# Mixing and layer 1 of a graph network: score products in halves of the array, W1 centred, shared places, fewer products behind each hyperedge block

## Chip, cores and metric

The kernel runs on one core of one Trainium2 chip. The metric is the device time of one execution in microseconds. Fast executions of the same kernel mostly agree within about 0.3%, so a difference of a few microseconds needs several rounds of both kernels on the same chip. For engines I use the names of the profile: PE (TensorE), DVE (VectorE), ACT (ScalarE), POOL (GpSimd), SP (the engine that issues most loads and stores here).

## The reference, cut to what matters

Eight batches of 2048 nodes with 64 features pass through four residual layers, each followed by a layernorm. The change touches the end of layer 0 and layer 1:

```python
# layer 0, hypergraph attention: industry = (adj / deg) @ (x @ W_ind); g = a mix over hyperedges
def attn_scores(f):
    return jnp.tanh(f @ fcW + fcb) @ av
pair = jnp.stack([industry, g], axis=2)
coefs2 = jax.nn.softmax(attn_scores(pair), axis=-1)
out = jnp.einsum('bnk,bnkf->bnf', coefs2, pair)
x = _layernorm(x + out)
# layer 1
A_td = A + jnp.eye(n); dinv = jax.lax.rsqrt(jnp.sum(A_td, axis=1))
H = jnp.einsum('bmd,nm->bnd', X, dinv[:, None] * A_td * dinv[None, :])
x = _layernorm(x + jnp.einsum('bnd,kd->bnk', H, W))
```

I call the choice between `industry` and `g` **mixing**. A softmax over two entries needs only the difference of the two scores.

## The kernel before

Batches lie in pairs: 128 partitions hold two batches of 64 features, so there are NP = 4 pairs, and 2048 nodes make NCH = 4 column groups of 512. Mixing therefore has 16 steps. PE's instructions are kept in program order. A generator, `filler`, gives the big adjacency products one by one, and `fill(n)` places n of them between the small products of a latency-bound stage: first behind the hyperedge blocks, then in mixing. It yields 576 products for layer 0 and then 640 for layer 1.

```python
# hyperedge stage: 57 blocks (t, s), three products each, seven fillers behind each
pz = pps.tile([P, C], F32, tag="mm", name="pz", bufs=3)
for i, (l, r) in enumerate(((ident_r, both[0]), (ident_r, both[1]), (ohs[s], tab2))):
    mm(pz, lhsT=l, rhs=r, start=i == 0, stop=i == 2)
if s == 0 and t + 1 < NT:
    fill(3)
    now = begin(t + 1)
fill(7)
...
def mix_parts(i):
    ...
    mm(pi, lhsT=bd_ind, rhs=ut, start=True, stop=True)           # 128 x 512, float32
    nc.vector.tensor_tensor(inds[i], pi, inv_row[:, cols(c)], ALU.mult)
    ...                                                          # pg: four transposes of g
    nc.scalar.activation(gts[i], pg, AF.Identity, bias=-1.0)

def mix_scores(i):
    for b in range(2):
        t1 = []
        for src in (inds[i], gts[i]):
            mm(pf, lhsT=fcz[:, b, :], rhs=src, start=True, stop=True)  # half of fcz's rows are zero
            nc.scalar.activation(t1[-1], pf, AF.Tanh, bias=fcb_col)
        nc.gpsimd.tensor_tensor(t1[0], t1[0], t1[1], ALU.subtract)
        tts[i].append(t1[0])

def mix_weigh(i):
    for b in range(2):
        mm(pd, lhsT=avz[:, b, :], rhs=tts[i][b], start=b == 0, stop=b == 1)  # half of avz's columns are zero
    nc.scalar.activation(th, pd, AF.Tanh, scale=0.5)
    nc.vector.tensor_tensor(ind, ind, gt, ALU.subtract)
    nc.vector.scalar_tensor_tensor(ind, th, 1.0, ind, op0=ALU.add, op1=ALU.mult)
    nc.vector.scalar_tensor_tensor(ind, ind, 0.5, gt, op0=ALU.mult, op1=ALU.add)

def mix_end(i):
    ...                                # pt: four transposes, add x, layernorm, store x1
def l1_parts(p, c):                    # layer 1's input, scaled and split in two float32r parts
    nc.vector.tensor_tensor(y, y, dinv[:, wide(c), None].to_broadcast([P, JT, P]), ALU.mult)
    part[c] = split(lp, y, f"v{c}", 1, [P, JT, P])
...
for i in range(steps + 1):
    k = 10 if i > NCH else 8
    ...                                # parts(i), weigh(i-1), scores(i), end(i-1), fill(k) after each
    if i == NCH:                       # the rest of layer 0's products, then start layer 1
        for _ in filler:
            pass
        ...
```

## Time and profile before

| | before |
|---|---|
| median of three runs, us | 2214.5 |
| PE busy, share of the span | 89% |
| DVE / ACT / POOL busy | 50% / 18% / 21% |
| stretch that the change touches | about 88 to 655 us |

A share of busy time is an average over stages. The prediction below therefore reads the stages one by one; it explains the columns of its rows where they first appear.

### The profile page before, as it was taken

To read this page: it belongs to the slowest core of one execution; us is meant where nothing else is said; L and a number is where in the kernel's file an instruction comes from. 1 tells how busy PE (TensorE), PEld (TensorE's weight loads), DVE (VectorE), ACT (ScalarE), POOL (GpSimd) and SP (SyncE) were. 2 spreads that over 40 slices of the span, in tenths; PEclk is the share of its full clock that TensorE was granted. 3 is DMA by queue.
4 is the path that set the end of the run, shared out by engine and by line. 5 is a ranking of instruction groups with operands and counts; after the bars stand their busy time and mean duration, and the time that the engine had idled before them with its cause. 6 is when DMAs were issued, how large, how long until landed. Compare 5 with 4: busy or idle time off the path is not lost. (4 is left out here: it accounts for less than half of the span.)

```text
span 2213.6 us, 19723 instructions
## 1 busy us (share of the span) xinstructions
PE 1972.6 (89%) x7292; PEld 1277.5 (58%) x7292; DVE 1112.3 (50%) x1825; ACT 405.9 (18%) x794; POOL 474.8 (21%) x420
## 2 busy tenths in 40 slices
PE   5799889898849999799999999999896999989994
PEld 3577656565634444474465456456445786877773
DVE  5579746666432232218846864772783233332322
ACT  1355433323111111010010010001001112212110
POOL 2368623434223333100100110110110010110102
PEclk8799989999869999999999999999998999999997
DMA  7823333231300000100000000000001112121110
GB/s 261 278 78 100 114 108 109 93 99 63 114 12 0 19 19 19 43 1 8 8 5 5 10 5 3 8 10 0 10 5 42 39 26 56 39 52 39 47 30 21
DMA packets 73241, 110.59 MB, mean 50 GB/s; under 512 B 26784, under 2 KB 35008, under 8 KB 70512
## 3 DMA queue, kind: packets, MB, share of 16 engines
q1 hardware_dynamic: 62304, 73.66, 11.3%
q0 software_dynamic: 5088, 25.89, 3.4%
q10 hardware_dynamic: 5744, 9.70, 1.2%
q8 instruction: 59, 0.97, 0.2%
q14 instruction: 46, 0.38, 0.1%
HBM read 79.27 MB, written 29.95 MB: 49 GB/s over the span
## 5 line engine op out<-in xcount | busy, mean ns | idle before, releaser
L1048 PE MATMUL py<-wp,xg 128*128 128x512 f32 x1024 | 448.4, 597 | 8.5 <-DVE fcav L1053 5.8
L1048 PEld LDWEIGHTS py<-wp,xg 128*128 128x128 f32 x1024 | 193.6, 191 | 254.4 <-issue 215.9
L173 PE MATMUL u<-adj,hi 128*128 128x512 f32 x768 | 256.7, 416 | 0.0
L173 PE MATMUL u<-adj,lo 128*128 128x512 f32 x768 | 247.5, 402 | 0.0
L995 PE MATMUL u<-pt,xn 128*128 128x512 f32 x512 | 227.9, 603 | 9.0 <-DVE u L1004 7.8
L1053 DVE TENSOR_TENSOR fcav<-py,emb_n 128x512 f32<-128x512 f32 x256 | 177.1, 692 | 51.9 <-PE py L1048 37.0
L1054 DVE TENSOR_REDUCE r<-fcav 128x32 f32<-128x512 f32 x256 | 175.4, 685 | 8.1
L995 PEld LDWEIGHTS u<-pt,xn 128*128 128x128 f32 x512 | 97.2, 193 | 131.4 <-issue 114.7
L678 PE MATMUL u<-adj,vh 128*128 128x512 f32 x512 | 158.2, 408 | 14.6 <-ACT vh L168 10.8
L173 PEld LDWEIGHTS u<-adj,hi 128*128 128x128 f32 x768 | 143.4, 190 | 40.9 <-issue 11.2
L173 PEld LDWEIGHTS u<-adj,lo 128*128 128x128 f32 x768 | 145.1, 191 | 34.0
L1056 POOL TENSOR_TENSOR r<-r,bias 128x256 f32<-128x256 f32 x32 | 23.4, 730 | 634.9 <-DVE r L1054 634.9
L156 POOL TENSOR_TENSOR ln_r<-ln_e,neg_half 128x8 f32<-128x8 f32 x64 | 106.9, 1670 | 223.4 <-DVE ln_e L154 219.5
L678 PE MATMUL u<-adj,vl 128*128 128x512 f32 x512 | 152.1, 398 | 0.0
L989 DVE TENSOR_SCALAR pt<-pt 128x512 f32<-128x512 f32 x64 | 48.8, 780 | 173.2 <-ACT pt L988 171.7
L1144 DVE SCALAR_TENSOR_TENSOR fcav<-fcav,ar 128x512 f32<-128x512 f32 x64 | 44.3, 692 | 177.4 <-ACT ar L1143 177.2
L678 PEld LDWEIGHTS u<-adj,vh 128*128 128x128 f32 x512 | 96.1, 189 | 45.0 <-ACT vh L168 12.3
L993 POOL TENSOR_TENSOR acc<-acc,pt 128x512 f32<-128x512 f32 x60 | 79.6, 1327 | 163.8 <-DVE pt L989 161.0
L1126 POOL TENSOR_TENSOR r<-r,xn 128x512 f32<-128x512 f32 x16 | 20.5, 1280 | 433.8 <-DVE r L1125 433.8
L678 PEld LDWEIGHTS u<-adj,vl 128*128 128x128 f32 x512 | 96.4, 189 | 22.1 <-issue 0.7
L150 ACT ACTIVATE r<-ln_c 128x512 f32<-128x512 f32 x64 | 40.3, 630 | 264.5 <-DVE ln_c L146 249.6
L1143 ACT CAST ar<-fcav 128x512 fp32r<-128x512 f32 x64 | 39.7, 621 | 213.8 <-DMA fcav<-in_adj_t 144.8
(342 smaller groups left out, 2736.6 us busy)
## 6 DMA issues: line engine op xcount, KB each, us to landing
adj<-in_adj_t POOLq DMA_DIRECT2D x16, 1024.0 KB, 8.2
fcav<-in_adj_t SPq DMA_DIRECT2D x64, 256.0 KB, 2.9
x_hbm<-r SPq DMA_DIRECT2D x28, 256.0 KB, 2.1
hs_hbm<-st ACTq DMA_DIRECT2D x16, 292.0 KB, 5.6
xt<-in_x_t SPq DMA_DIRECT2D x16, 256.0 KB, 4.6
xc<-in_x_n SPq DMA_DIRECT2D x16, 256.0 KB, 2.9
u_hbm<-ut SPq DMA_DIRECT2D x16, 256.0 KB, 2.5
gn<-gs_hbm SPq DMA_DIRECT2D x16, 256.0 KB, 3.7
```

Of the source, the lines that this page charges most:

```text
L150: nc.scalar.activation(r, xc, AF.Square)
L156: nc.gpsimd.tensor_tensor(rstd, vare, neg_half[:, :groups], ALU.pow)
L173: tc.keep_in_program_order(nc.tensor.matmul(*args, **kw))
L678: nc.tensor.matmul(u[c], lhsT=half[:, j, :], rhs=adj[t][:, cols(c)], start=t == 0 and i == 0, stop=ends and not own,)
L989: nc.vector.tensor_scalar(pt, pt, 1.0, None, op0=ALU.max)
L993: nc.gpsimd.tensor_tensor(acc, acc, pt, ALU.add)
L995: nc.tensor.matmul(u[p], lhsT=xn[p][:, t, :], rhs=pt, start=t == 0, stop=t == NT - 1)
L1048: nc.tensor.matmul(py.rearrange("p o d -> p (o d)"), lhsT=xg[b][:, q, cols(j, P)], rhs=wp[:, q, cols(k)], start=q == 0, stop=q == 1,)
L1053: nc.vector.tensor_tensor(pr, py, e_b, ALU.mult)
L1054: nc.vector.tensor_reduce(r[:, j, b, cols(k, OH)], pr, AX.X, ALU.add)
L1143: nc.scalar.copy(ar, a)
L1144: nc.vector.scalar_tensor_tensor(a, a, 1.0, ar.bitcast(F32), op0=ALU.mult, op1=ALU.not_equal, accum_out=left[:, t, k:k + 1],)
```

## The change

Its intent: less PE time for the scores, and fewer holes in mixing.

- `pf` uses 64 rows of the array for each batch of a pair, and `pd` 64 columns, so that the two batches' products can run side by side.
- Five instead of seven fillers stand behind each hyperedge block; the others remain for mixing. The last two tiles change places.
- The columns of W1 are centred, so that what layer 1 adds has mean zero, and its layernorm needs no mean.
- Three passes go from DVE to POOL: ind - gt, the addition of g (now to x and early, as x + g, called the residual below), the scaling of layer 1's input. The factor of one half goes into the DVE pass that adds the residual. The copies of `ut` that DVE made go to ACT.
- Loads of mixing get a pool of their own, opened before the hyperedge stage ends; layer 1 uses the places of layer 0's split parts and can start quarter by quarter.

```diff
@@ layernorm: with centred=True no mean, no subtraction
@@ hyperedge stage
-        for t in range(NT):
+        tiles = [*range(NT - 2), NT - 1, NT - 2]
+        for k, t in enumerate(tiles):
...
-                fill(7)
+                fill(5)
@@ mixing
-        ut = mp.tile([P, C], F32, tag="ut0", name="ut0", bufs=2)
+            uts[i] = mp0.tile([P, C], F32, tag="ut0", name="ut0", bufs=2)
...
+        nc.gpsimd.tensor_tensor(rs[i], rs[i], gn, ALU.add)
 
     def mix_scores(i):
-        for b in range(2):
-            t1 = []
-            for src in (inds[i], gts[i]):
+        t1 = []
+        for src in (inds[i], gts[i]):
+            for b in range(2):
+                s = slice(b * F, (b + 1) * F)
-                mm(pf, lhsT=fcz[:, b, :], rhs=src, start=True, stop=True)
+                mm(pf, lhsT=fc2[s, :], rhs=src[s, :], start=True, stop=True)
...
+        for b in range(2):
+            nc.gpsimd.tensor_tensor(t1[b], t1[b], t1[2 + b], ALU.subtract)
+        tts[i] = t1[0:2]
+        nc.gpsimd.tensor_tensor(inds[i], inds[i], gts[i], ALU.subtract)
 
     def mix_weigh(i):
-            mm(pd, lhsT=avz[:, b, :], rhs=tts[i][b], start=b == 0, stop=b == 1)
+            mm(pd[b * F:(b + 1) * F, :], lhsT=av2, rhs=tts[i][b], start=True, stop=True)
-        nc.vector.tensor_tensor(ind, ind, gt, ALU.subtract)
-        nc.vector.scalar_tensor_tensor(ind, th, 1.0, ind, op0=ALU.add, op1=ALU.mult)
-        nc.vector.scalar_tensor_tensor(ind, ind, 0.5, gt, op0=ALU.mult, op1=ALU.add)
+        nc.vector.scalar_tensor_tensor(inds[i], th, 1.0, inds[i], op0=ALU.add, op1=ALU.mult)
@@ layer 1: w1_m is the mean of each row of bd_w1's blocks
+        nc.vector.tensor_scalar(bd_w1[s, s], bd_w1[s, s], w1_m[s], None, op0=ALU.subtract)
-        nc.vector.tensor_tensor(y, y, dinv[:, wide(c), None].to_broadcast([P, JT, P]), ALU.mult)
-        part[c] = split(lp, y, f"v{c}", 1, [P, JT, P])
+        nc.gpsimd.tensor_tensor(y, y, dinv[:, wide(c), None].to_broadcast([P, JT, P]), ALU.mult)
+        part[p, c] = split(va, y, f"v{c}", 1, [P, JT, P])
@@ the order of a step: scores(i), end(i-1), load and ind and g of i+1, weigh(i), fill(k) after each
-        k = 10 if i > NCH else 8
+        k = 9 if i > NCH else 8
-        if i == NCH:
-            for _ in filler:
-                pass
```

More of the change, by code (lines that the diff above doesn't have):

```diff
@@ L139, in to_rows, with layernorm @@
         return t
-    def layernorm(pool, r, dst, groups=2 * JT):
-        mean = pool.tile([P, groups], F32, tag="ln_m", name="ln_m", bufs=2)
-        nc.vector.tensor_reduce(mean, r, AX.X, ALU.add)
+    def layernorm(pool, r, dst, groups=2 * JT, centred=False):
         xc = pool.tile([P, groups, F], F32, tag="ln_c", name="ln_c", bufs=1)
-        nc.vector.scalar_tensor_tensor(
-            xc, mean[:, :, None].to_broadcast([P, groups, F]), -1.0 / F, r,
-            op0=ALU.mult, op1=ALU.add,
-        )
-        nc.scalar.activation(r, xc, AF.Square)
+        if centred:
+            squares, xc = xc, r
+        else:
+            mean = pool.tile([P, groups], F32, tag="ln_m", name="ln_m", bufs=2)
+            nc.vector.tensor_reduce(mean, r, AX.X, ALU.add)
+            nc.vector.scalar_tensor_tensor(
+                xc, mean[:, :, None].to_broadcast([P, groups, F]), -1.0 / F, r,
+                op0=ALU.mult, op1=ALU.add,
+            )
+            squares = r
+        nc.scalar.activation(squares, xc, AF.Square)
         var = pool.tile([P, groups], F32, tag="ln_v", name="ln_v", bufs=2)
-        nc.vector.tensor_reduce(var, r, AX.X, ALU.add)
+        nc.vector.tensor_reduce(var, squares, AX.X, ALU.add)
         vare = pool.tile([P, groups], F32, tag="ln_e", name="ln_e", bufs=2)
@@ L190, in tile_gnn_fast @@
     fcav = const.tile([P, 2, 2, P], F32, name="fcav")
-    fcz, avz = fcav[:, 0], fcav[:, 1]
+    fc2, av2 = fcav[:, 0, 0], fcav[:, 0, 1, 0:F]
     bd_ind = const.tile([P, P], F32, name="bd_ind")
@@ L273, in tile_gnn_fast @@
     xc, part = {}, {}
+    mixed, free = set(), set()
     def fetch(p, c):
@@ L338, in products @@
                             yield
+                    if p == NP - 1 and g == 1 and t % JT == JT - 1:
+                        first_parts(t // JT, free)
                     if p + 1 < NP and t % JT == JT - 1:
@@ L354, in fill, with first_parts @@
         for _ in range(n):
-            next(filler, None)
+            if next(filler, None) == "wait":
+                break
+    def first_parts(c, where):
+        where.add(c)
+        if c in mixed and c in free:
+            l1_parts(0, c)
     ph_scope = ExitStack()
@@ L398, in tile_gnn_fast @@
             nc.gpsimd.dma_start(dst, v.rearrange("(n o) -> n o", o=1))
-        for t in (fcz, bd_ind):
-            nc.gpsimd.memset(t, 0.0)
+        nc.gpsimd.memset(bd_ind, 0.0)
         for b in range(2):
             s = slice(b * F, (b + 1) * F)
-            nc.gpsimd.dma_start(fcz[s, b, :], fc_w)
+            nc.gpsimd.dma_start(fc2[s, :], fc_w)
             nc.gpsimd.dma_start(bd_ind[s, s], w_ind)
-        nc.gpsimd.memset(avz, 0.0)
         age = hy.tile([P, F], F32, name="age")
@@ L519, in tile_gnn_fast @@
         nc.vector.scalar_tensor_tensor(order, po[:, 0, :], float(P), olo, op0=ALU.mult, op1=ALU.add)
-        for b in range(2):
-            s = slice(b * F, (b + 1) * F)
-            nc.vector.tensor_copy(avz[:, b, s], av_col.to_broadcast([P, F]))
+        nc.vector.tensor_copy(av2, av_col.to_broadcast([P, F]))
         so_scope.close()
@@ L622, in tile_gnn_fast @@
         for b in range(2):
+            s = slice(b * F, (b + 1) * F)
             pf = pps.tile([P, 2, P], F32, tag="sm", name="pf", bufs=2)
-            mm(pf, lhsT=fcz[:, b, :], rhs=het, start=True, stop=True)
+            mm(pf, lhsT=fc2[s, :], rhs=het[s], start=True, stop=True)
             nc.scalar.activation(tf[:, b], pf, AF.Tanh, bias=fcb_col)
@@ L665, in tile_gnn_fast @@
         ta_scope.close()
+    mix_scope = ExitStack()
+    mp0 = mix_scope.enter_context(tc.tile_pool(name="mix0", bufs=1, side="right"))
     def product(pool, psum, chunk, plus_identity=False):
@@ L696, in begin @@
         def begin(t):
-            fetch_rows(t + 2)
+            k = tiles.index(t)
+            for ahead in tiles[k + 2:k + 3]:
+                fetch_rows(ahead)
             hrow = hrows.pop(t)
@@ L717, in begin @@
             return S, both, ohs, R, co
+        tiles = [*range(NT - 2), NT - 1, NT - 2]
         now = begin(0)
-        slots(1, pps, "mm", 3)
-        for t in range(NT):
+        slots(tiles[1], pps, "mm", 3)
+        for k, t in enumerate(tiles):
             S, both, ohs, R, co = now
@@ L727, in tile_gnn_fast @@
                     mm(pz, lhsT=l, rhs=r, start=i == 0, stop=i == 2)
-                if s == 0 and t + 1 < NT:
+                if s == 0 and k + 1 < NT:
                     fill(3)
-                    now = begin(t + 1)
-                fill(7)
-                if s == max(0, S - 5) and t + 2 < NT:
-                    slots(t + 2, pps, "mm", 3)
+                    now = begin(tiles[k + 1])
+                fill(5)
+                if s == max(0, S - 5) and k + 2 < NT:
+                    slots(tiles[k + 2], pps, "mm", 3)
                 z = pz.rearrange("p (b f) -> p b f", f=F)
@@ L768, in tick, with mix_load, mix_ind, mix_g @@
             pending.pop(0)[1]()
-    mix_scope = ExitStack()
+    lp_scope = ExitStack()
+    lp = lp_scope.enter_context(tc.tile_pool(name="l1", bufs=1))
     mp = mix_scope.enter_context(tc.tile_pool(name="mix", bufs=1, side="right"))
-    inv_row = mp.tile([P, N], F32, name="inv_row")
-    nc.scalar.dma_start(inv_row, inv_hbm[:])
     lps_scope = ExitStack()
     lps = lps_scope.enter_context(tc.tile_pool(name="l1_ps", bufs=1, space=PSUM))
+    bd_w1 = on_diagonal(lp, w1_t, "bd_w1")
+    w1_m = lp.tile([P, 1], F32, name="w1_m")
+    nc.vector.tensor_reduce(w1_m, bd_w1, AX.X, ALU.add)
+    nc.vector.tensor_scalar(w1_m, w1_m, 1.0 / F, None, op0=ALU.mult)
+    for b in range(2):
+        s = slice(b * F, (b + 1) * F)
+        nc.vector.tensor_scalar(bd_w1[s, s], bd_w1[s, s], w1_m[s], None, op0=ALU.subtract)
     def wide(c):
         return slice(c * JT, (c + 1) * JT)
-    gts, inds, tts = {}, {}, {}
-    def mix_parts(i):
+    uts, invs, gts, inds, tts, rs = {}, {}, {}, {}, {}, {}
+    xn, done = [], [0] * NP
+    steps = NP * NCH
+    def mix_load(i):
+        if i < steps:
+            p, c = divmod(i, NCH)
+            uts[i] = mp0.tile([P, C], F32, tag="ut0", name="ut0", bufs=2)
+            nc.sync.dma_start(uts[i], u0_hbm[p][:, cols(c)])
+            invs[i] = mp0.tile([P, C], F32, tag="inv0", name="inv0", bufs=2)
+            nc.sync.dma_start(invs[i], inv_hbm[:, cols(c)])
+    def mix_ind(i):
+        pi = lps.tile([P, C], F32, tag="mm", name="pi", bufs=4)
+        mm(pi, lhsT=bd_ind, rhs=uts.pop(i), start=True, stop=True)
+        inds[i] = mp.tile([P, C], F32, tag="ind", name="ind", bufs=3)
+        nc.vector.tensor_tensor(inds[i], pi, invs.pop(i), ALU.mult)
+    def mix_g(i):
         p, c = divmod(i, NCH)
@@ L788, in mix_parts @@
         )
-        ut = mp.tile([P, C], F32, tag="ut0", name="ut0", bufs=2)
-        nc.sync.dma_start(ut, u0_hbm[p][:, cols(c)])
-        pi = lps.tile([P, C], F32, tag="mm", name="pi", bufs=4)
-        mm(pi, lhsT=bd_ind, rhs=ut, start=True, stop=True)
-        inds[i] = mp.tile([P, C], F32, tag="ind", name="ind", bufs=2)
-        nc.vector.tensor_tensor(inds[i], pi, inv_row[:, cols(c)], ALU.mult)
+        rs[i] = mp.tile([P, JT, P], F32, tag="r", name="r", bufs=2)
+        load_x(rs[i], p, c)
         pg = lps.tile([P, C], F32, tag="mm", name="pg", bufs=4)
@@ L799, in mix_parts @@
         nc.scalar.activation(gts[i], pg, AF.Identity, bias=-1.0)
+        nc.gpsimd.tensor_tensor(rs[i], rs[i], gn, ALU.add)
     def mix_scores(i):
-        tts[i] = []
-        for b in range(2):
-            t1 = []
-            for src in (inds[i], gts[i]):
+        t1 = []
+        for src in (inds[i], gts[i]):
+            for b in range(2):
+                s = slice(b * F, (b + 1) * F)
                 pf = lps.tile([P, C], F32, tag="mm", name="pf", bufs=4)
-                mm(pf, lhsT=fcz[:, b, :], rhs=src, start=True, stop=True)
+                mm(pf, lhsT=fc2[s, :], rhs=src[s, :], start=True, stop=True)
                 t1.append(mp.tile([P, C], F32, tag="t1", name="t1", bufs=4))
                 nc.scalar.activation(t1[-1], pf, AF.Tanh, bias=fcb_col)
-            nc.gpsimd.tensor_tensor(t1[0], t1[0], t1[1], ALU.subtract)
-            tts[i].append(t1[0])
+        for b in range(2):
+            nc.gpsimd.tensor_tensor(t1[b], t1[b], t1[2 + b], ALU.subtract)
+        tts[i] = t1[0:2]
+        nc.gpsimd.tensor_tensor(inds[i], inds[i], gts[i], ALU.subtract)
     def mix_weigh(i):
@@ L817, in mix_weigh @@
         for b in range(2):
-            mm(pd, lhsT=avz[:, b, :], rhs=tts[i][b], start=b == 0, stop=b == 1)
+            mm(pd[b * F:(b + 1) * F, :], lhsT=av2, rhs=tts[i][b], start=True, stop=True)
         th = mp.tile([P, C], F32, tag="th", name="th", bufs=1)
         nc.scalar.activation(th, pd, AF.Tanh, scale=0.5)
-        ind, gt = inds[i], gts[i]
-        nc.vector.tensor_tensor(ind, ind, gt, ALU.subtract)
-        nc.vector.scalar_tensor_tensor(ind, th, 1.0, ind, op0=ALU.add, op1=ALU.mult)
-        nc.vector.scalar_tensor_tensor(ind, ind, 0.5, gt, op0=ALU.mult, op1=ALU.add)
+        nc.vector.scalar_tensor_tensor(inds[i], th, 1.0, inds[i], op0=ALU.add, op1=ALU.mult)
     def mix_end(i):
         p, c = divmod(i, NCH)
-        r = mp.tile([P, JT, P], F32, tag="r", name="r", bufs=2)
-        load_x(r, p, c)
+        r = rs.pop(i)
         pt = lps.tile([P, C], F32, tag="mm", name="pt", bufs=4)
@@ L832, in mix_end @@
             transpose(pt[:, cols(j, P)], inds[i][:, cols(j, P)])
-        nc.vector.tensor_tensor(r, pt.rearrange("p (t f) -> p t f", f=P), r, ALU.add)
+        nc.vector.scalar_tensor_tensor(
+            r, pt.rearrange("p (t f) -> p t f", f=P), 0.5, r, op0=ALU.mult, op1=ALU.add
+        )
         layernorm(mp, grouped(r), grouped(r))
         nc.sync.dma_start(x1_hbm[p][:, wide(c), :], r)
+        if p == 0:
+            first_parts(c, mixed)
     def l1_parts(p, c):
-        y = lp.tile([P, JT, P], F32, tag="y", name="y", bufs=2)
+        y = staged("y")
         nc.sync.dma_start(y, x1_hbm[p][:, wide(c), :])
-        nc.vector.tensor_tensor(y, y, dinv[:, wide(c), None].to_broadcast([P, JT, P]), ALU.mult)
-        part[c] = split(lp, y, f"v{c}", 1, [P, JT, P])
+        nc.gpsimd.tensor_tensor(y, y, dinv[:, wide(c), None].to_broadcast([P, JT, P]), ALU.mult)
+        part[p, c] = split(va, y, f"v{c}", 1, [P, JT, P])
     def l1_end(p, c, ut):
@@ L846, in l1_end @@
             mm(po[:, j, :], lhsT=ut[:, cols(j, P)], rhs=bd_w1, start=True, stop=True)
-        x1 = lp.tile([P, JT, P], F32, tag="y", name="x1", bufs=2)
+        x1 = staged("x1")
         nc.sync.dma_start(x1, x1_hbm[p][:, wide(c), :])
@@ L852, in l1_end, with load_xn @@
         if p == NP - 1:
-            layernorm(lp, grouped(r), grouped(xn[p][:, wide(c), :]))
+            layernorm(lp, grouped(r), grouped(xn[p][:, wide(c), :]), centred=True)
         else:
-            layernorm(lp, grouped(r), grouped(r))
+            layernorm(lp, grouped(r), grouped(r), centred=True)
             nc.sync.dma_start(x2_hbm[p][:, wide(c), :], r)
+        done[p] += 1
+        load_xn()
+    def load_xn():
+        for p in range(NP - 1):
+            if xn and done[p] == NCH:
+                done[p] = 0
+                nc.scalar.dma_start(xn[p], x2_hbm[p][:])
     def layer1(p):
@@ L861, in layer1 @@
             own = (2 * g, 2 * g + 1)
-            ug = pph.tile([P, 2, C], F32, tag="ph", name="u1", bufs=2)
-            u = {c: ug[:, c % 2, :] for c in own}
+            ug = None
             for t in range(NT):
+                while (p, t // JT) not in part:
+                    yield "wait"
+                if ug is None:
+                    ug = pph.tile([P, 2, C], F32, tag="ph", name="u1", bufs=2)
+                    u = {c: ug[:, c % 2, :] for c in own}
                 for i in range(2):
@@ L867, in layer1 @@
                         end = t == NT - 1 and i == 1
+                        half = part[p, t // JT][i][:, t % JT, :]
                         mm(
-                            u[c], lhsT=part[t // JT][i][:, t % JT, :], rhs=adj[t][:, cols(c)],
+                            u[c], lhsT=half, rhs=adj[t][:, cols(c)],
                             start=t == 0 and i == 0, stop=end and t // JT != c,
@@ L874, in layer1 @@
                         if t // JT == c:
-                            mm(
-                                u[c][:, cols(t % JT, P)], lhsT=part[c][i][:, t % JT, :], rhs=ident_r,
-                                start=False, stop=end,
-                            )
+                            mm(u[c][:, cols(t % JT, P)], lhsT=half, rhs=ident_r, start=False, stop=end)
                             tick()
@@ L883, in layer1 @@
             for k, c in enumerate(own):
-                ut = lp.tile([P, C], F32, tag="ut", name="ut", bufs=2)
-                if k == 0:
-                    nc.scalar.copy(ut, u[c])
-                else:
-                    nc.vector.tensor_copy(ut, u[c])
+                ut = va.tile([P, C], F32, tag="ut", name="ut", bufs=2)
+                nc.scalar.copy(ut, u[c])
                 later(6 + 8 * k, lambda p=p, c=c, ut=ut: l1_end(p, c, ut))
     def all_pairs():
+        yield from remaining
         for p in range(NP):
             yield from layer1(p)
-    fill(36)
-    steps = NP * NCH
-    for i in range(steps + 1):
-        k = 10 if i > NCH else 8
-        if i < steps:
-            mix_parts(i)
-            fill(k)
-        if i > 0:
-            mix_weigh(i - 1)
-            fill(k)
+    remaining = filler
+    filler = all_pairs()
+    mix_load(0)
+    mix_load(1)
+    fill(24)
+    mix_ind(0)
+    fill(12)
+    mix_g(0)
+    fill(4)
+    for i in range(steps + 1):
+        k = 9 if i > NCH else 8
         if i < steps:
@@ L911, in tile_gnn_fast @@
             fill(k)
-        if i == NCH:
-            for _ in filler:
-                pass
-            va_scope.close()
-            l1_scope = ExitStack()
-            lp = l1_scope.enter_context(tc.tile_pool(name="l1", bufs=1))
-            bd_w1 = on_diagonal(lp, w1_t, "bd_w1")
-            for c in range(NCH):
-                l1_parts(0, c)
-            filler = all_pairs()
+        if i + 1 < steps:
+            mix_load(i + 2)
+            mix_ind(i + 1)
+            mix_g(i + 1)
+            fill(k)
+        if i < steps:
+            mix_weigh(i)
+            fill(k)
     mix_scope.close()
     xnp = ctx.enter_context(tc.tile_pool(name="xnp", bufs=1, side="right"))
-    xn = [xnp.tile([P, NT, P], F32, name=f"xn{p}") for p in range(NP)]
-    for p in range(2):
-        nc.scalar.dma_start(xn[p], x2_hbm[p][:])
-    fill(40)
-    nc.scalar.dma_start(xn[2], x2_hbm[2][:])
+    xn += [xnp.tile([P, NT, P], F32, name=f"xn{p}") for p in range(NP)]
+    load_xn()
     for _ in filler:
@@ L932, in tile_gnn_fast @@
         tick()
-    l1_scope.close()
+    lp_scope.close()
+    va_scope.close()
     lps_scope.close()
```

## The prediction

> **What bounds the kernel now.** I read the page first, then the table of stages (busy time per engine in stretches that I cut where named tiles start and stop), then the waits of PE, then single stretches of the timeline. The change touches the span only from about 88 us (the hyperedge blocks, the first `pz`) to 616 us (the last layer 1 product), so I ask what bounds that stretch. In the stage view the columns are start:end, length, then busy us (and instructions) of PE, PEld, DVE, ACT, POOL, then the granted clock, DMA share and GB/s.
>
> ```profile
> 88.00:264.00 176.00, 163.34 (x709) 128.88 (x709) 146.43 (x242) 87.10 (x221) 125.46 (x98) 0.96 0.36 124
> 264.00:337.00 73.00, 59.65 (x196) 36.02 (x196) 29.46 (x39) 22.23 (x36) 19.81 (x15) 0.88 0.35 116
> 337.00:565.00 228.00, 199.10 (x817) 136.72 (x816) 149.51 (x220) 66.30 (x111) 85.81 (x57) 0.95 0.28 89
> 565.00:616.00 51.00, 40.90 (x202) 33.90 (x200) 18.51 (x32) 4.31 (x7) 13.33 (x10) 0.90 0.30 109
> 616.00:655.00 39.00, 12.65 (x41) 9.64 (x42) 16.41 (x21) 8.10 (x10) 9.41 (x7) 0.53 0.13 17
> ```
>
> The rows are: hyperedge blocks; mixing with the last of `x W_ind`'s adjacency products; mixing with layer 1; layer 1 alone; the passage to layer 2. PE is the busiest engine in the first four, but from 264 to 616 it idles 52 of 352 us (length less busy: 13.4 + 28.9 + 10.1), and the clock of 0.88 to 0.95 says that it ran part of the rest at half rate. What ended that idle time, by the waits of PE from 264 to 616 us (total, times, longest):
>
> ```profile
> PE pt L176 <- DVE ind L824: 16.3, 4, 8.0
> PE po L173 <- ACT ut L886: 9.7, 4, 6.4
> PE pf L173 <- DVE ind L794: 8.1, 4, 4.1
> PE pi L173 <- DMA ut<-u_hbm: 8.1, 1, 8.1
> PE pi L173 <- ACT t L810: 5.7, 2, 2.9
> ```
>
> So mixing is PE work with holes: PE executes in program order and meets a mixing product whose input VectorE has not finished. VectorE itself is busy 149.5 of 228 us; in the timeline it waits in its own queue for the layernorm's GpSimd power (idle before L157: 36.9 us from 337 to 565).
>
> The unit costs, from the timeline. A float32r product of 512 columns comes every 0.233 us, a full float32 product is two instructions and takes 0.86 us:
>
> ```profile
> 171.40 0.63 PE L173 MATMUL ug<-adj,v2l 128*128 128x512 f32 x2
> 171.87 0.40 PE L173 MATMUL ug<-adj,v2h 128*128 128x512 f32 x1
> ...
> 496.00 1.02 PE L173 MATMUL pf<-gt,fcav 128*128 128x512 f32 x2
> 496.86 1.02 PE L173 MATMUL pf<-ind,fcav 128*128 128x512 f32 x2
> 497.71 1.02 PE L173 MATMUL pf<-gt,fcav 128*128 128x512 f32 x2
> ```
>
> Starts of the `pf` pairs are 0.86 apart, though each pair shows 1.02 with its tail. The `ug` pair takes 171.87 - 171.40 = 0.47. Score products thus cost nearly four times an adjacency product, and half of their contraction rows are zeros (`fcz` holds the weights of one batch half only).
>
> **What the Trainium skill says.** (1) "TensorEngine Tiling (Array Packing)", Key Properties: tiles of a divided array work independently, but changing the mode drains the engine. This trace has a case, the aggregation `pagg`, whose outputs are two halves of 64 columns of the array:
>
> ```profile
> 43.33 0.66 PE L567 MATMUL pagg<-ex,m_n 128*64 128x260 f32 x4
> 43.91 0.97 PEld L535 LDWEIGHTS ph<-bd,xt 128*128 128x128 f32 x8 [0.39 <-issue]
> ```
>
> Two products (four instructions) of 260 columns, next load 0.58 after the first start. Scaling 0.86 by 260/512 gives 0.44 for one, 0.87 for two in a row: so the halves do overlap, with about 0.14 of overhead. That is halves by columns; for halves by rows no row of this trace speaks, the skill's "TensorE: Matmul & The Clock Gate", Part 3, describes both as concurrent. (2) The same page, Why this matters for your kernels, warns of PE gaps over about 3 us since the clock then halves; the trace agrees (after the 4.06 us wait at 514.9 the next `pf` pair took 1.91 rather than 1.02). (3) "SBUF — State Buffer", Who interferes with whom: a VectorE instruction with two SBUF inputs excludes a GpSimd one that reads SBUF. The trace agrees: L822 (two SBUF inputs) averages 1285 ns, L794 (one from PSUM) 683.
>
> **The change, part by part.**
>
> *Scores in halves.* Per mixing step (16 of them) four `pf` products become 64-row ones in two overlapping pairs, and the two `pd` products become 64-column ones that overlap. From 4 x 0.86 = 3.43 to 2 x (0.86 + 0.07) = 1.85; from 1.72 to 0.93. I use 0.07 per pair-half as half of `pagg`'s 0.14, scaled for the mode change. Saved: 1.58 + 0.79 = 2.4 us a step, 38 us of PE in all, on the engine that sets the pace. Elements for ScalarE are unchanged.
>
> *Fewer products behind a hyperedge block (7 to 5).* 57 blocks, so 114 products of 0.233 = 26.6 us of PE leave the hyperedge stage and must be done in mixing: no PE work vanishes. The block period is 2.32 to 2.33 us now, which is exactly (3 + 7) x 0.233; with 8 products it would be 1.87. But VectorE needs 0.69 + 0.69 for the two passes over `pz` and 0.69 to 1.2 for the third, about 2.1 us, plus 14 us for the 16 tiles' coefficients (0.9 each). So VectorE becomes the bound there: busy 146 us plus some 10 of gaps. I expect the stage to take 156 instead of 176: 20 us earlier.
>
> *The seam.* The 8.1 us wait for `ut` at the first mixing step came because its buffers lie in places freed only at the end of the hyperedge stage; the change gives them a pool of their own, opened before, and reads the inverse degrees in pieces. Swapping the last two tiles gives the last scatter a longer cover. 40 products (9.3 us) and `pi`, `pg` stand before the first scores, and I allow 2 us for gathered rows: 244 + 9.3 + 1.2 + 2, first scores at 257 (now the first `pi` starts at 278, scores some 3 later).
>
> *Mixing.* Moved off VectorE: the difference ind - gt (L822, 20.6 us), the dinv scaling (L840, 12.4), L824 (13.1; its half factor goes into the add that follows); with W1 centred, layer 1's layernorm loses mean and centring (16 x (0.68 + 0.72) = 22 us). Together 68 us of VectorE over mixing and layer 1. GpSimd gets three more passes of about 1.3 us a step, 62 us. Layer 1 starts as soon as its first quarter is there, instead of after a stop with nothing to fill the holes.
> The step now: a step with layer 1 has 40 filler products (0.199 on average: 512 of 0.233 and 128 of 0.055), 8.0, one `po` group 0.86 and mixing 6.7 (`pi` 0.86, `pg` and `pt` 0.36 each, `pf`, `pd`): 15.6 us; `pi` starts from 355.9 to 525.2 give 18.8, so 3.2 are lost to idle time and cold clock. After: 36 x 0.199 = 7.2, `po` 0.8, mixing 4.3: 12.3. I put the loss at 2.7, as VectorE is lighter but the step shorter: 15.0. The first five steps have 32 full products: 7.5 + 4.3 + 2 = 13.8.
>
> *The sum.* 257 + 5 x 13.8 = 326; + 11 x 15.0 = 491. Then what is left of the filler: of 1216 products 362 go by the end of the hyperedge stage, 40 at the seam, 24 in the first step, 4 x 32, then 11 x 36 and 9; 257 are left, 257 x 0.199 + six `po` groups = 56.5, plus 6 for waits like the present one for `ut` behind a queued load on ScalarE: 554 against 616. The centred layernorm makes the last tail 1.4 shorter. Total 63 us: 2214.5 - 63 = 2151. Nothing after 655 changes.
>
> Cross-check by losses from hyperedge end to 616: now 271 us of PE work in 352 (81 lost); then 259 in 310 (51 lost).
>
> **Rivals.** (a) *GpSimd becomes the bound of mixing.* Per step with layer 1 it gets two score differences 2.9, ind - gt and the residual 2.6, power 1.67, and 0.9 times (scaling 1.3, residual 1.3, power 1.67): about 11 of 12.3 us, before it is shut out by VectorE's two-input instructions (some 3 us a step). Step 17: 22 us more, 2173, within 2%. For it: these sums; against: its chain has slack of a third of a step. (b) *Halves by rows do not overlap*, or the change of mode eats it: 16 x 1.6 = 25 us are not saved, 2176. Against: `pagg`. (c) *Losses stay 81 us*, as waits in VectorE's queue only move: 30 more, 2181. (d) *The holes close*: the new order gives scores to weighing three fills, so losses fall to 25, 2125. (e) Hyperedge stage bound as now by latency: time moves, 10 to 20 more.
>
> **Range and chances.** Two of (a), (b), (c), (e) in part are worth 37, (d) 26 and a hyperedge stage at PE's pace another 6 to 7 with what follows: 2112 to 2188. The 2% line is 2170, 19 above my estimate: faster 0.74, same 0.24, slower 0.02.
>
> **What would show it.** `pf` starting in pairs within some ns, four in about 1.9 us; first `pf` near 257; `pz` blocks near 2.1 us with VectorE over 90% busy; `pi` spacing near 15 after the first five; GpSimd under 90% busy in mixing (else (a)); the last layer 1 product near 554. I am wrong if `pf` starts stay 0.4 apart, if GpSimd ends PE's waits, or if the first scores still wait for a load.

## The result, and the profile after

| | before | after |
|---|---|---|
| median of four runs, us | 2216.2 | 2177.2 |
| ratio, with 95% interval | | 0.982 (0.980 to 0.984) |
| PE / DVE / ACT / POOL busy | 89 / 50 / 18 / 21% | 90 / 49 / 19 / 25% |

A ratio here is the mean time of one kernel's fast runs over that of the kernel before in the same rounds, so it is not quite the ratio of the medians. The gain is 39 us.

The table below is worked out from the start times of single instructions in the two traces. "Hyperedge" is from the first to the last first product of a block (`pz`), "seam" to the first `pi`, "mixing" to the last transpose `pt`, "tail" to the last adjacency product of layer 1, "passage" to the first product of the next layer's softmax. The idle time of PE stands behind the slash. The tail grew because products that stood behind hyperedge blocks before are left for it now.

| stage, us | before | after |
|---|---|---|
| hyperedge | 171.1 / 12.7 | 163.9 / 28.7 |
| seam | 18.9 / 8.1 | 7.4 / 0.0 |
| mixing | 277.5 / 34.2 | 245.6 / 18.8 |
| tail | 55.3 / 7.8 | 68.8 / 3.6 |
| passage | 38.2 / 28.7 | 33.5 / 24.0 |
| all after it | 1564.2 | 1566.2 |

These are one profile each. A stage that an edit leaves alone repeats within about 3 us (the hyperedge stage took 163.9 to 166.9 us in eight profiles with five fillers and three buffers of rows), but the stretch before the first `pz` varies from 85.4 to 95.0 us over all profiles. So I compare stages, and for the whole time the ratios.

The kernel after, by stages, columns as before (hyperedge; mixing with layer 0's products; mixing with layer 1; layer 1 alone; passage):

```profile
88.00:252.00 164.00, 135.31 (x575) 103.67 (x574) 136.82 (x235) 81.84 (x211) 118.85 (x92) 0.96 0.37 127
252.00:336.00 84.00, 81.76 (x341) 52.17 (x340) 34.72 (x53) 31.38 (x54) 48.34 (x37) 0.98 0.41 138
336.00:505.00 169.00, 152.45 (x665) 97.48 (x664) 89.46 (x125) 57.84 (x99) 111.07 (x79) 0.95 0.35 114
505.00:574.00 69.00, 65.33 (x323) 54.07 (x321) 24.20 (x35) 10.09 (x18) 24.39 (x18) 0.98 0.30 107
574.00:612.00 38.00, 14.11 (x56) 11.38 (x57) 15.36 (x19) 9.11 (x12) 10.43 (x8) 0.57 0.13 17
```

Layer 0's part of mixing is now almost solid PE work (81.8 of 84), where before PE was busy for 59.7 of 73 us. In the hyperedge stage PE and DVE are now equally busy (135 and 137 of 164), and neither is full.

The waits of PE after, from 251 to 600 us:

```profile
PE pb L1023 <- issue: 13.8, 1, 13.8
PE pf L178 <- DVE ind L823: 6.6, 2, 5.0
PE po L178 <- ACT ut L940: 4.7, 4, 2.1
PE pt L181 <- DVE ind L865: 3.0, 2, 2.9
```

The wait for `ut` at the first `pi` (8.1) is gone, and that of `pt` fell from 16.3 to 3.0.

The score products after, in the timeline of PE (start, length to the end of the last, line, names, columns of the array, count of instructions):

```profile
401.07 1.07 PE L178 MATMUL pd<-t,fcav 128*64 128x512 f32 x2
402.73 1.07 PE L178 MATMUL pd<-t,fcav 128*64 128x512 f32 x2 [0.58 <-POOL t L853]
...
405.66 1.13 PE L178 MATMUL pf<-ind,fcav 64*128 64x512 f32 x4
406.62 1.02 PE L178 MATMUL pf<-gt,fcav 64*128 64x512 f32 x4
...
417.24 1.08 PE L178 MATMUL pd<-t,fcav 128*64 128x512 f32 x4
```

The two halves of `pf` start 3 to 7 ns apart, in pairs. But the `pd` pair comes in two kinds: at 417.24 all four instructions together, at 401.07 two, a wait for POOL's second score difference, and then the other two. To measure a group's whole cost I take the time from its first start to the second start behind it, less 0.233 us for the product between. The group of four `pf` then takes 2.02 us (before 3.43), and `pd` 0.94 to 1.17 in nine steps and 1.55 to 2.77 in the other seven (before mostly 1.71). This measure misses one thing: the first start of a group in halves comes 0.32 us behind the start of the 512-column product ahead of it, where 0.23 is usual (0.15 instead of 0.06 behind a 128-column one). All groups at the full clock that PE did not wait for show this 0.09, and none in the kernel before or e1 does: four `pf` cost 2.11, an overlapping `pd` 1.21.

### The profile page after: what moved, and what is told of

It reads as the page before. It is cut to its first block, busy times and chain, and to the rows that moved or that the text cites. A ratio compares the mean times of both kernels' runs of the same rounds, so it can differ in the third digit from the quotient of the medians.

```text
span 2173.2 us, 19790 instructions
## 1 busy us (share of the span) xinstructions
PE 1949.9 (90%) x7292; PEld 1253.0 (58%) x7292; DVE 1055.3 (49%) x1740; ACT 407.9 (19%) x802; POOL 534.1 (25%) x466
## 5 line engine op out<-in xcount | busy, mean ns | idle before, releaser
L1038 ACT ACTIVATE pt<-s 128x512 f32<-128x512 f32 x64 | 34.0, 602 | 232.4 <-PE s L1036 190.9
```

The source lines that it names most:

```text
L1038: nc.scalar.activation(pt, s, AF.Exp)
```

## The experiments

Each experiment changes the kernel after, except the second. The times are of three rounds, the last of five, beside runs of the kernel before; differences from the kernel after are worked out from the ratios, times 2217 us. One run of the kernel before at 2586 us counts as slow and is in no ratio.

| run | ratio (95% interval) | against the kernel after, us |
|---|---|---|
| after | 0.9821 (0.9802 to 0.9840) | |
| e1_full_array | 0.9897 (0.9866 to 0.9927) | +17 |
| e2_only_halves | 0.9925 (0.9897 to 0.9953) | (before less 17) |
| e3_seven_behind | 1.0137 (1.0105 to 1.0168) | +70 |
| e4_uncentred | 0.9866 (0.9837 to 0.9895) | +10 |
| e5_seven_capped | 0.9804 (0.9773 to 0.9836) | -4 |
| e6_pinned | 0.9837 (0.9802 to 0.9873) | +4 |
| e7_deeper_gather | 0.9825 (0.9786 to 0.9865) | +1 |
| e8_shared_loads | 0.9840 (0.9799 to 0.9881) | +4 |
| e9_vector_back | 0.9801 (0.9774 to 0.9828) | -4 |
| e10_second_diff | 0.9808 (0.9775 to 0.9842) | -3 |
| e11_eleven_fill | 0.9881 (0.9854 to 0.9908) | +13 |
| e12_combined | 0.9814 (0.9794 to 0.9835) | -2 |

Where the interval overlaps that of the kernel after broadly (e5 to e10, e12), the times alone show no difference, and I use these runs for what their traces show.

My theory was that PE sets the pace of mixing, so that the halves are most of the gain; e1 and e2 will give them 17 of 39 us, less than half. The rivals were that the closed holes are, or the products moved out of the hyperedge stage, or the lighter DVE.

### e1: scores on the whole array again

```diff
-                mm(pf, lhsT=fc2[s, :], rhs=src[s, :], start=True, stop=True)
+                mm(pf, lhsT=fcz[:, b, :], rhs=src, start=True, stop=True)
-            mm(pd[b * F:(b + 1) * F, :], lhsT=av2, rhs=tts[i][b], start=True, stop=True)
+            mm(pd, lhsT=avz[:, b, :], rhs=tts[i][b], start=b == 0, stop=b == 1)
```

> The changed kernel with only the scores put back on the whole array (zero-padded weights, as before). In the changed kernel's trace four pf products take 1.92 us and the pd pair 1.0 where it overlaps, against 3.43 and 1.72. Theory (PE sets the pace of mixing, so what halves save is nearly all of the gain): 16 x 2.2 = 35 us come back, near 2212. Rival (the gain comes from closed holes and the earlier start of layer 1, the halves run into other waits): at most 15 back, near 2190.

Measured: 17 us slower, half of what I expected and just over the rival's 15: neither holds as stated. Mixing takes 262.7 us instead of 245.6. (The edit also puts back the set-up of the padded weights and a small `pf` ahead of the hyperedge blocks. The first `pz` starts at 95.0 us here, the latest of all profiles; with the scatter given above, one profile doesn't say whether the edit did that.) The timeline of PE in this run:

```profile
274.63 1.88 PE L178 MATMUL pf<-ind,fcav 128*128 128x512 f32 x4
276.35 1.88 PE L178 MATMUL pf<-gt,fcav 128*128 128x512 f32 x4
283.10 1.88 PE L178 MATMUL pd<-t,fcav 128*128 128x512 f32 x4
```

By the measure above with the 0.09, `pf` costs 3.43 again (16 x 1.32 = 21 us more), while `pd` averages 1.85 against 1.69 in the kernel after: only 16 x 0.16 = 3 us, because seven of its sixteen pairs do not overlap. That makes 24 us of PE. The rest of the way to 17 is in the clock: the idle time of PE in mixing stayed at 19.8, but the mean clock there was 0.99 instead of 0.96, so less ran at the half rate. An estimate from these figures, 0.03 of 246 us, is 7 us, the whole difference; one profile each doesn't settle its size.

### e2: the kernel before with the halves alone

```diff
 (the kernel before, with fc2, av2 and the order of mix_scores of the change)
```

> The kernel before with only the scores in halves of the array, everything else as it was. Theory: mixing of before lost 81 us to holes, so part of the saved PE time turns into longer holes: 20 to 30 us gained of 35, near 2190. Rival of closed holes: under 10 gained, above 2206. Rival that the halves alone are the whole change: 39 gained, 2177.

Measured: 17 us faster than the kernel before, the same as e1 says from the other side. The score halves are thus 17 of the 39 us and do not depend on the rest of the change. The theory's range was 20 to 30, the rival's under 10: neither hit. As in e1, `pd` is a part of the miss: eight of its sixteen pairs cost 1.4 us or more, although POOL has none of the moved passes in this kernel. The idle time of PE in mixing also grew, from 34.2 to 37.5 us, as the theory said.

### e3: seven products behind each block

```diff
-                fill(5)
+                fill(7)
```
(With a guard: layer 1's input of the next pair is loaded only when it is mixed; without it layer 1 could read what is not yet written. The guard stands in e5, e11 and e12 too.)

> The changed kernel with 7 instead of 5 products behind each hyperedge block (and a guard on layer 1's loads that changes no order in the changed kernel itself). Theory: the hyperedge stage ends near 260 instead of 252 us, 114 fewer products are left for mixing, whose steps 2 to 5 then have nothing to fill their holes: between 5 faster and 10 slower than 2177. Rival (the stage is worth what it took off PE): 27 slower, 2204. Second rival (VectorE-bound hyperedge stage makes 5 too few): 15 faster, 2162.

Measured: 70 us slower than the kernel after and slower than the kernel before, outside every expectation. The timeline of PE, only the lines that begin with a wait:

```profile
321.39 1.22 PE L178 MATMUL u<-adj,v1h 128*128 128x512 f32 x2 [7.42 <-ACT v1h L173]
...
341.84 1.22 PE L178 MATMUL u<-adj,v2h 128*128 128x512 f32 x2 [10.01 <-ACT v2h L173]
...
365.32 1.22 PE L178 MATMUL u<-adj,v3h 128*128 128x512 f32 x2 [13.80 <-ACT v3h L173]
```

All waits of PE for the four quarters' first halves add up to 56 us here. With 114 fillers used up earlier, layer 1's products come up while the quarters `v1`, `v2`, `v3` of their input are still in the making. They are put into PE's queue as soon as the instructions that make a quarter are issued, and PE, in program order, stands still for the whole latency of store, load, scaling and split. So a filler helps only when its own inputs are long ready; the five also keep layer 1 behind mixing.

### e5: seven products, but mixing's count held

```diff
-                fill(5)
+                fill(7)
+ fill(n) in mixing only raises a target; products are given while fewer than the target were given,
+ and the target starts 114 lower than what has been given; the guard of e3
```

> 7 products behind each hyperedge block again, but now the fillers of mixing count the 114 products already done: none are given until the changed kernel's own count is reached, so layer 1 never runs ahead of mixing as it did with seven alone (there PE waited 56 us for ScalarE's first halves of layer 1). Theory: the hyperedge stage ends 8 us later, the first three mixing steps have nothing to fill and take 9 to 11 instead of 12.7 us, the seam is 9 shorter: between 3 faster and 10 slower than the changed kernel. Rival (moving products is where the gain lies): over 15 slower.

Measured: 0.9804, not to be told from the kernel after. The hyperedge stage takes 172.7 us (after: 163.9) with PE idle for 13.9 of it, mixing 239.7 (after: 245.6), the seam 4.3 (7.4). Moving 26.6 us of PE work out of the hyperedge stage shortened that by 9 and lengthened mixing and seam by as much: as a part of the change it was worth nothing that these runs can see. What five in place of seven does is keep fillers in stock; with a count held as here that is not needed, without it e3 shows the price.

### e7: gathered rows fetched a tile earlier

```diff
-            hrows[t] = hy.tile([P, HROW], F32, tag="hrow", name="hrow", bufs=3)
+            hrows[t] = hy.tile([P, HROW], F32, tag="hrow", name="hrow", bufs=4)
-            for ahead in tiles[k + 2:k + 3]:
+            for ahead in tiles[k + 2:k + 4]:
```

> The changed kernel with four instead of three buffers of gathered rows, fetched three tiles ahead. Theory (the hyperedge stage lost its gain to latencies, of which the gather's is the largest wait of PE, 8.8 us): the stage 4 to 8 us shorter than 164. Rival (VectorE bounds the stage, 137 of 164 busy): under 2.

It asks why the hyperedge stage gained 7 us rather than 20. The largest waits of PE there in the kernel after (75 to 264 us) were:

```profile
PE pslot L181 <- DMA hrow<-hs_hbm,order: 8.8, 5, 5.0
PE pinv L181 <- DVE deg L315: 4.9, 1, 4.9
PE ug L178 <- DMA adj<-in_adj_t: 3.6, 5, 0.9
PE pz L178 <- DVE R L728: 3.1, 3, 1.8
```

With four buffers the stage took 160.8 instead of 163.9 us and the wait for rows 4.3 instead of 8.8, but the first mixing step then waited 6.3 us for its rows (kernel after: 2.1), and the total stayed. Since eight profiles with three buffers took 163.9 to 166.9, the 3 us are just outside the scatter. They lie between my theory and the rival. Within a tile the blocks follow each other every 1.85 to 1.95 us, as eight products of 0.233 want; the time goes at the starts of tiles, where two blocks lie 3 to 8 us apart, with waits of several kinds. What bounds the stage is left open beyond this: no single one of these waits.

### e4: W1 not centred

```diff
-            layernorm(lp, grouped(r), grouped(r), centred=True)
+            layernorm(lp, grouped(r), grouped(r))
- (and the subtraction of w1_m from bd_w1)
```

> The changed kernel with W1 as it is and layer 1's full layernorm, 16 x 1.4 = 22 us more on VectorE. Theory: VectorE is off the path, busy about 53% of mixing, so 2 to 6 us slower, 2179 to 2183, 1.4 of it in the tail before layer 2. Rival (VectorE's queue sets the holes): 15 to 20 slower, 2194.

Measured: 10 us slower (the two intervals just overlap), between theory and rival. The traces show where: mixing 252.0 instead of 245.6, and the passage 38.0 instead of 33.5. The passage is one wait of PE for the last two layernorms and what is behind them; here before, after and e4 in this order, each from that kernel's waits of PE:

```profile
PE pb L973 <- issue: 18.4, 1, 18.4
```
```profile
PE pb L1023 <- issue: 13.8, 1, 13.8
```
```profile
PE pb L1017 <- issue: 18.2, 1, 18.2
```

In the tail nothing is left to hide DVE, and two layernorms follow each other there: two means and two subtractions of about 0.69 us each are 2.8 of the 4.5 us; I put the rest down to the hops between engines.

### e8: mixing's loads in the mixing pool

```diff
-            uts[i] = mp0.tile([P, C], F32, tag="ut0", name="ut0", bufs=2)
+            uts[i] = mp.tile([P, C], F32, tag="ut0", name="ut0", bufs=2)
-            invs[i] = mp0.tile([P, C], F32, tag="inv0", name="inv0", bufs=2)
+            invs[i] = mp.tile([P, C], F32, tag="inv0", name="inv0", bufs=2)
```

> The changed kernel with the buffers of ut and of the inverse degrees in the mixing pool again, whose places come free at the end of the hyperedge stage. Theory: the wait of the first pi returns less what 24 products cover: 3 to 8 us slower. Rival (24 products cover it all): within 1.

Measured: 4 us by the ratios, which alone would not show it. The waits of PE in this run name the old cause:

```profile
PE pi L178 <- DMA ut<-u_hbm: 5.8, 1, 5.8
```

The seam takes 13.4 instead of 7.4 us. The stage fits the theory's 3 to 8, and the rival falls: 24 products hide only a part of the wait, and the separate pool the rest.

### e9, e10 and e6: why `pd` overlaps in nine steps only

The timeline of POOL in the kernel after shows what stands ahead of the score differences (`t<-t,t`):

```profile
335.32 1.29 POOL L839 TENSOR_TENSOR r<-r,gn 128x512 f32<-128x512 f32 x1 [2.71 <-DVE r L873]
336.57 1.49 POOL L884 TENSOR_TENSOR y<-y,dinv 128x512 f32<-128x512 f32 x1
338.02 2.52 POOL L853 TENSOR_TENSOR t<-t,t 128x512 f32<-128x512 f32 x2
```

and the timeline of PE what followed:

```profile
339.52 2.15 PE L178 MATMUL pd<-t,fcav 128*64 128x512 f32 x4
```

The tanh of the scores were done at 333.3 (the last started at 332.62), but POOL was standing before the residual of the next step, then did the scaling of layer 1's input, both passes that the change moved to it; the second difference ended at 340.5, a microsecond after `pd` had begun with the first. Over the whole of mixing the residual's wait for its load of x is POOL's longest (waits of POOL from 259 to 505 us):

```profile
POOL r L839 <- DMA r<-in_x_n: 28.9, 9, 5.7
```

e9 puts the three moved passes back on DVE:

```diff
-        nc.gpsimd.tensor_tensor(inds[i], inds[i], gts[i], ALU.subtract)
+        nc.vector.tensor_tensor(inds[i], inds[i], gts[i], ALU.subtract)
 (and likewise the residual and the scaling by dinv)
```

> The changed kernel with its three moved passes (ind - gt, the residual, the scaling of layer 1's input) on VectorE again: GpSimd loses some 62 us, VectorE gains 16 x about 2.7 = 44. Theory (GpSimd's queue is what makes the second score difference late in 7 of 16 steps): pd near 1.12 in 13 or more steps; VectorE, then near 75% busy in mixing, takes part of it back: between 6 faster and 3 slower than the changed kernel. Rival (the move to GpSimd is a part of the gain): 8 to 15 slower.

e10 gives only the second score difference to DVE:

```diff
-            nc.gpsimd.tensor_tensor(t1[b], t1[b], t1[2 + b], ALU.subtract)
+            (nc.gpsimd, nc.vector)[b].tensor_tensor(t1[b], t1[b], t1[2 + b], ALU.subtract)
```

> The changed kernel with the score difference of the second batch on VectorE, that of the first on GpSimd, so that the two do not follow each other. Theory: pd 1.12 in 13 or more steps, the 7 steps of 1.6 to 2.8 us lose about 1.0 each, 5 to 8 us faster, near 2170. Rival (VectorE in its own order is as late): pd late as often, within 2 us.

Both do for `pd` what was expected: 0.94 to 1.12 us in 15 (e9) and 16 (e10) of 16 steps. The view of the tile `pd` lists what its readers and writers waited for (us, times); the line for the score differences in the kernel after and then in e10:

```profile
  POOL t L853: 9.2, 14
```
```profile
  POOL t L853: 0.4, 1
```

Of the 9.2 us 8.3 are waits of the weight loads (PEld), 0.9 of PE itself; what a late pair costs PE is the longer time that it takes. So the lateness of POOL's second difference was the cause of the lost overlap. Yet neither run is measurably faster (-4 and -3 us). In e10 mixing is 241.5 us, 4 less; about 8 us of PE work were saved (16 x 0.5), and the longest step of the kernel after, from the tenth to the eleventh `pi`, still takes 19.8 us (after: 20.2), and the longest of e10 20.6. e9 also says that moving three passes to POOL was no part of the gain that these runs can see: POOL is busy 71 instead of 111 of 169 us in mixing with layer 1 and DVE 104 instead of 89, and the time is the same.

e6 tried to keep POOL's score differences, ind - gt and residual in program order:

```diff
-        nc.gpsimd.tensor_tensor(rs[i], rs[i], gn, ALU.add)
+        tc.keep_in_program_order(nc.gpsimd.tensor_tensor(rs[i], rs[i], gn, ALU.add))
 (and likewise the score differences and ind - gt)
```

> The changed kernel with GpSimd's score differences, ind - gt and residual kept in the order of the program. In the changed kernel's trace the residual of the next step, which waits for its load, stands ahead of the score differences in 12 of 16 steps; the pd pair overlaps (1.12 us) in 9 steps only and takes 1.6 to 2.8 in the other 7. Theory: pd 1.12 in 14 or more steps, and 5 to 10 us faster, 2167 to 2172. Rival (PE's own work and VectorE set the steps): within 2 us.

It failed: `pd` was still late in eight steps (1.5 to 2.5 us), since unpinned passes stepped in between, and `pf` waited longer for `ind` (10.0 us instead of 6.6). The run is 4 us slower by the ratios, within the noise.

### e11: eleven fillers in each place

```diff
-        k = 9 if i > NCH else 8
+        k = 11 if i > NCH else 8
```

> The changed kernel with 11 instead of 9 products in each of the four places of a mixing step after the fifth, so 88 fewer remain after mixing. Theory (the late steps are as long as VectorE's and GpSimd's chains, 15.8 against 12.3 us of PE work): the steps stay near 16 to 16.5 while the tail loses 88 x 0.2 = 17 us: 6 to 12 faster. Rival (steps are PE-bound with jitter): steps grow by 1.6, no change within 2. Third: layer 1 reaches the quarters of the next pair before they are mixed, and PE waits for them: slower.

Measured: 13 us slower. The tail shrank from 68.8 to 51.4 us as planned, but mixing grew from 245.6 to 274.1: its later steps take 14 to 27 us. PE idles for 25.6 us in it (18.8). The rise of 28 us is more than the 88 products (17 us): the third case of the expectation or a like one, new waits for `po` and `pf` (5.4 and 5.7 us each once). I have not followed it further. More fillers in these places thus cost time; fewer were not tried.

### e12: the two best together

```diff
 e5 and e10 in one kernel
```

> The changed kernel with two findings joined: the second score difference on VectorE, and 7 products behind each hyperedge block with mixing's fillers held to the changed kernel's own count (which had 9 of 16 pd pairs late). Theory: all pd pairs at about 1.12, 6 to 10 us faster than the changed kernel, ratio to the kernel before 0.977 to 0.980. Rival (what pd saves turns up as waits elsewhere, as mostly with the second difference alone): 0.980 to 0.983.

Measured over five rounds: 0.9814, so the rival holds: not to be told from the kernel after. Mixing is 234.7 us, 5 less than in e5, but with more idle time (32.3 against 28.2) at the same clock (0.935 and 0.936). `pd` overlaps in fourteen of the sixteen steps. No version that I tried beats the kernel after clearly.

## Why the prediction was right or wrong

The time, 2177, lies in the range (2112 to 2188), 26 us above the estimate of 2151. The chance put on "faster by over 2%" was too high at 0.74; the measured gain is 1.8%. (One sum of the range doesn't come out: 26 and 6 to 7 below 2151 is 2118, not 2112.) Point by point:

- **The sum, last layer 1 product "near 554": 576.6, so 22.6 late.** The first scores came 10.5 us late; the five steps behind them took 62.1 instead of 69, 6.9 less; the eleven later steps and the rest of the filler took 246.9 instead of 227.5, 19.4 more. In the last part the steps are about 0.8 longer each than foreseen; behind the last `pt` 275 products were left where the sum has 266, and PE took 71.9 us to the end of `po`, of which 4.2 idle. So the range held partly by luck: the early steps made good some of what the others lost.
- **PE with holes bounds mixing: right.** From the hyperedge stage's end to layer 1's end PE lost 81 us before by the prediction's count of its work; I foresaw 51. With the halves' saving corrected to 24 us, PE work after is 259 + 14 = 273 us in 322 (251.6 to 573.5): 49 lost. In the traces the idle time alone fell from 50 to 22 us over seam, mixing and tail.
- **"Scores in halves", 38 us: the mechanism right, the size wrong.** Halves by rows do overlap (rival b fell), but the term was mis-sized twice. From the first start to the next product's start, the measure that I took from `pagg`, four `pf` take 1.92 (I had 1.85) and an overlapping `pd` 1.01 (0.93). That measure misses the 0.09 ahead of the group, and the product behind it, which takes 0.33 instead of 0.23. And `pd` saved 0.16 a step rather than 0.79, mostly because POOL delivers the second difference late in seven steps (e9, e10). That is 24 us of PE, of which 17 arrived in the time (e1, e2).
- **"I expect the stage to take 156 instead of 176", 20 us: wrong.** The hyperedge stage gave 7. I had made DVE the bound, over 90% busy at 2.1 us a block; it is 83% busy, blocks within a tile run at 1.9, and latencies at the starts of tiles hold the stage. My reading of the block period left these starts out: 2.32 to 2.33 holds within a tile only, the mean distance of blocks before was 171.1 / 56 = 3.05. So 41 us (171.1 less 56 x 2.33) lay at the starts before, and 60 (163.9 less 56 x 1.86) after: of 26 us won within the tiles 19 were lost there. That nothing is lost by moving the products was right as a matter of PE work; e5 shows that nothing is won either.
- **The seam: right.** 7.4 instead of 18.9 us; 8.1 of it is the wait for `ut`, of which 5.8 return without the load's own pool (e8); some 3.3 are fourteen products fewer ahead of the first `pi` (29 instead of 43), which are only moved. The first scores came at 267.5, not 257, because the stage before ended 8 us later than I put it and the gathered rows a little later: PE waited 2.1 us for them (`pg`, on the load of `gn`), which is the sign "the first scores still wait for a load" in the size that I had allowed for.
- **Mixing steps: near.** The steps from the first to the sixth `pi` average 12.9 (I had 13.8), those from the seventh to the last 15.8 (15.0).
- **Centring, "1.4 shorter" in the last tail: too small.** The passage is 4.7 shorter, and e4 finds 10 us for centring in all. It is the last two layernorms that the term mis-sized: I had counted one pair of passes and forgotten that two layernorms run one after the other where nothing hides them.
- **Layer 1 starting by quarters: not used.** The last product of layer 0 starts at 338.3 and the first of layer 1 at 338.6, when all four quarters are mixed. Before, 27 us (310.2 to 337.3) lay between the two. The stock of fillers closed this hole, not the early start.
- **Rival (a), POOL as the bound: half right.** POOL is busy 66% in mixing with layer 1, so it isn't the bound, and e9 gains nothing measurable. But its queue is what spoilt `pd`.
- **VectorE shut out by GpSimd: shown, but not by the two means in the prediction,** which would differ too if L822 were simply slower. The single instructions show it: of the sixteen of L822 in the kernel before seven took 0.68 us and nine 1.6 to 1.8, and each of the nine ran beside a GpSimd instruction for over 1 us. About half of its 20.6 us was thus waiting.

What the experiments account for: halves 17, centring 10, the loads' pool 4 of 39 us. Only the halves are measured from both sides; the 4 are within the noise, and the sum takes it that the parts add. The other 8 are not tested one by one; the swap of the last two tiles, the copies on ACT, the early start of layer 1 and the new order of the steps are in them.

## What to carry to other kernels

Two products in halves of the array save time only if both halves' inputs are ready together; see that the engine which makes the second input isn't held by a waiting instruction in front of it. A filler product is one only when its own inputs are long there: count how many are left in stock, and keep the consumer well behind the producer. A VectorE pass that is hidden in the middle of a kernel can be on the path at the end of a stage, so price it there.

## What the Trainium skill lacked or had wrong

- "TensorEngine Tiling (Array Packing)", Key Properties, says that a change of mode drains the engine, without a figure. Here four full float32 products in two halves by rows took 2.11 us with what comes before and behind them, where 4 x 0.43 = 1.72 would be without a change, and two in halves by columns 1.21 where 0.86 would be: 0.35 to 0.4 us for each visit. These runs don't show how much of it is the drain.
- The same page, Theoretical Speedup, gives up to 2x for a dimension of 64 or less. That is an upper bound and not wrong; here it was 3.43 / 2.11 = 1.6x by rows and 1.71 / 1.21 = 1.4x by columns, for float32 products of 512 columns. The gain in the time was smaller still (17 us of 24).
- That page and "TensorE: Matmul & The Clock Gate", Part 3, don't say what happens when one half's operand is late: the pair then cost 1.55 to 2.77 us, mostly more than the 1.71 on the whole array.
